# A state-space block on one core: the first part of y moves behind the first chunk of the next step

## The chip, the core and the metric

The kernel runs on one core of one Trainium2 chip. A core has TensorE (PE, matrix multiplication, with PEld for its weight loads), VectorE (DVE), ScalarE (ACT), GpSimd (POOL) and SyncE (SP, which here only issues DMAs). All share an on-chip memory; TensorE writes its results to PSUM banks, of which this kernel uses eight. Each engine works through its own instructions in order and waits for the others at semaphores. The metric is the device time of one execution in microseconds, lower is better. Times are medians over runs of the same kernel; a profile is one execution recorded by the hardware.

## What is computed

The input x has 64 sequences of 32 positions and 512 channels. The block is

- a conditioning: a small network makes from `cond_128` a 32x32 mixing matrix for each sequence, which mixes the 32 positions of x;
- a state-space layer on the result, added to x:

```
proj = hidden @ in_proj_w.T            # gate z 4096, conv part x 4096, B 1024, C 1024, dt 64
xBC  = silu(causal_conv4(proj[conv part]))
dt   = softplus(dt + dt_bias);  dA = exp(-exp(A_log) * dt)
for t in range(32):                    # state per head: 64 x 128; 64 heads in 8 groups
    state = state * dA[t] + (dt[t] * x[t]) (outer) B[t]
    y[t]  = state . C[t]
y    = rmsnorm_per_group(y + D * x) * norm_weight * silu(z)
out  = y @ out_proj_w.T
```

- a grouped convolution over channels and a gated dense layer, added again.

The kernel doesn't step through the 32 positions. For one group of eight heads it forms `C.B` for all pairs of positions (the Gram matrix), multiplies it with the decay between the two positions and with dt, and so gets a 32x32 matrix per sequence and head, with which y is one small matrix product.

## The kernel before

The 64 sequences are cut in four tiles of 16 sequences (T = 0 to 3; 512 columns each), and the 64 heads in eight groups (g = 0 to 7). The main loop (L923) has 32 **steps**, i = 8 T + g, one for each tile and group. A step works on ten **chunks** of the input projection (ORDER, L346): B, C, then x and z alternately four times. `chunk(i, c)` (L417) orders the loads of weights some chunks ahead and the splitting of a later weight tile, and does one chunk: 12 matmuls of 128x512 into one PSUM bank (`mm_split`, L193: each product is formed from a high and a low part, three times four matmuls). `evict` (L448) empties the bank: for z ScalarE's silu (L452), for the others a bias on ScalarE (L459), three taps of the convolution on VectorE (L463), and ScalarE's silu in place (L471). `flip` (L473) transposes an x chunk on VectorE into `xs` (L478); the fourth, `flip(i, 3)`, comes after chunk 9.

Beside that `gram` and `gram_rows` (L534, L549) form the Gram matrix, `scan` (L511) the decay, and `decay` (L561) puts both together in `src`, the tile that the page also shows as `y<-src,xs`. Then y: `y_part(i, a, e)` (L577) does the blocks a to e of 16. A block is 8 matmuls of 32 rows and 64 columns, two for each of four PSUM banks; `y_part(i, 0, 8)`, the **first part**, takes the four banks and does 64 matmul pairs, 128 in the profile's count of matmuls and as many weight loads; `y_part(i, 8, 16)`, the **second part**, does the rest. Each block needs all four x chunks of `xs`.

Step i also finishes step j = i - 1. After chunk 1 comes the second part of y of j and `yend(j, 0..3)` (L594), which reads the four y banks on ScalarE (square, L600) and VectorE (times z, L602) and splits the result in a high and a low part (L613, L614); after chunks 5 to 8 come the four output products `outp` (L675) of j, with `wo`, the output weights, and `outp_end` (L691), which adds them to `acc`.

In the first eight steps the weights come raw from memory and are split in a high and a low part by ScalarE and GpSimd (`w_split`, L401; `wo_split`, L664), and stored for the later tiles; from step 8 on the split tiles are loaded. Steps 5, 6 and 7 (and 13 to 15, 21 to 23) also prepare the next tile: `attend` and `cond` (the conditioning), `dt_stage` (softplus and decay). At the first step of a tile `da_store` and `da_load` (L341, L482) write the decay rows to memory and read them back spread out, by DMAs of SyncE.

The order on TensorE and SyncE is the order in which the program is written (`manual_schedule`, L906). The order on VectorE, ScalarE and GpSimd is set by a planner that simulates the program, and the waits are put in by it. All accumulators but one come from a pool of seven PSUM banks (`bank`, L89), used in turn: an allocation waits until the seventh one before it has been read.

After the loop (L1034) the last step's second part, its outputs and the dense layer follow, interleaved with `unit`, pieces of the second convolution (`conv`, L787).

Of the kernel before, what the change touches and what calls it, by code (L numbers as in the profile page):

```python
# [32 lines left out]
def mamba_block_kernel(  # L33
# [55 lines left out]
    def bank(name, rows=P, cols=TOK):  # L89
        return ps.tile([rows, cols], F32, tag="mm", name=name, bufs=7)  # L90
# [102 lines left out]
    def mm_split(o, a_hi, a_lo, b_hi, b_lo, n):  # L193
        last = 3 * n - 1
        j = 0
        for a, b in ((a_hi, b_hi), (a_lo, b_hi), (a_hi, b_lo)):
            for k in range(n):
                nc.tensor.matmul(o, lhsT=a(k), rhs=b(k), start=j == 0, stop=j == last)  # L198
                j += 1
# [141 lines left out]
    def da_store(T):  # L341
        m = m_of.pop(T)
        for g in range(NG):
            nc.sync.dma_start(out=da_d[T][g], in_=m[g:P:NG])
# [51 lines left out]
    def w_ahead(n):  # L396
        while ahead[0] <= n + (5 if ahead[0] < 10 * NG else 4 if n < 10 * NG else 6):
            w_load(ahead[0])
            ahead[0] += 1

    def w_split(n):  # L401
        if n >= NG * 10:
            return
        w = raws.pop(n)
        t = w_tile(n)
        hi, lo = t[:, 0], t[:, 1]
        if len(w.shape) == 4:
            hi, lo = (v.rearrange("p k (q c) -> p k q c", q=4) for v in (hi, lo))
        nc.scalar.copy(hi, w)  # L409
        sub_of[n] = nc.gpsimd.tensor_tensor(lo, w, hi.bitcast(F32), ALU.subtract).ins  # L410
        splits[n] = t
# [5 lines left out]
    def chunk(i, c):  # L417
        n = 10 * i + c
        g = i % NG
        kind, k = ORDER[c]  # L420
        st = state[i]
        for m, t in keep:
            nc.sync.dma_start(out=wsp_d[m], in_=t.bitcast(F32))
        keep.clear()
        w_ahead(n)
        with tc.issue_after(exp_of[0] if n == 0 else cast_of[0]):
            w_split(n + 3)
        w2 = splits.pop(n)
        if i < NG:
            keep.append((n, w2))  # L430
        hi, lo = w2[:, 0], w2[:, 1]
        hid_hi, hid_lo = hid_of[i // NG]
        o = bank(f"mm{n}")
        mm_split(
            o,
            lambda q: hi[:, q, :],
            lambda q: lo[:, q, :],
            lambda q: hid_hi[:, q, :],
            lambda q: hid_lo[:, q, :],
            KC,  # L440
        )
        tag, bufs = {"B": ("B", 2), "C": ("C", 2), "x": ("x", 4), "z": ("z", 6)}[kind]
        t = sb.tile([P, TOK], F32, tag=tag, name=f"{kind}{n}", bufs=bufs)
        st[(kind, k)] = t
        with tc.issue_after(exp_of[0]) if n == 0 else nullcontext():
            evict(i, c, o, t)

    def evict(i, c, o, t):  # L448
        g = i % NG
        kind, k = ORDER[c]  # L450
        if kind == "z":
            nc.scalar.activation(t, o, AF.Silu)  # L452
        else:
            if kind == "x":
                taps, bias = xw[k][:, g, :], xb[k][:, g : g + 1]
            else:
                cc = chunk_id(g, kind, k) - 32
                taps, bias = convw_s[:, cc, :], convb_s[:, cc : cc + 1]
            nc.scalar.activation(t, o, AF.Identity, bias=bias, scale=taps[:, 3:4])  # L459
            ov = o.rearrange("p (b t) -> p b t", t=L)  # L460
            tv = t.rearrange("p (b t) -> p b t", t=L)
            for d in (1, 2, 3):
                nc.vector.scalar_tensor_tensor(  # L463
                    tv[:, :, d:],
                    ov[:, :, : L - d],
                    taps[:, 3 - d : 4 - d],
                    tv[:, :, d:],
                    ALU.mult,
                    ALU.add,
                )  # L470
            nc.scalar.activation(t, t, AF.Silu)  # L471
# [105 lines left out]
    def y_part(i, a, e):  # L577
        st = state[i]
        if a == 0:
            st["y"] = [bank(f"y{i}_{q}") for q in range(4)]  # L580
        for n in range(a, e):
            hh, b = divmod(n, 8)
            for f in range(2):
                for q in range(4):
                    r = slice(32 * q, 32 * q + 32)
                    nc.tensor.matmul(  # L586
                        st["y"][q][64 * f : 64 * f + 64, 32 * n : 32 * n + 32],
                        lhsT=st["xs"][r, n, 2 * f : 2 * f + 2].rearrange("p e x -> p (e x)"),
                        rhs=st["dec"][r, 2 * hh + f, b, :],
                        start=True,  # L590
                        stop=True,
                    )
# [71 lines left out]
    def wo_split():  # L664
        if wo_raw:
            t, k, w = wo_raw.pop(0)
            nc.scalar.copy(t[:, 0, k, :], w)  # L667
            nc.gpsimd.tensor_tensor(t[:, 1, k, :], w, t[:, 0, k, :].bitcast(F32), ALU.subtract)

    def wo_store():  # L670
        if wo_new:
            g, t, h = wo_new.pop(0)
            nc.sync.dma_start(out=wos_d[g][:, h], in_=t[:, h].bitcast(F32))
# [213 lines left out]
    def unit(n=1):  # L887
        for _ in range(n):
            units.pop(0)()
# [33 lines left out]
    for i in range(NI):  # L923
        j = i - 1
        T, g = divmod(i, NG)
        state[i] = {}
        late = 2 if i == 0 else 0

        def step_more():
            next(cond_steps, None)  # L930
            next(dt_steps, None)

        def inner(c):
            nonlocal wo_steps
            if c in (1, 2, 3, 4):
                if c < 4:
                    wo_split()
                next(wo_steps, None)
            if c in (5, 6):
                wo_store()  # L940
            if i == 0 and c == 6:
                da_rows()
                scan(0)
            if i == 0 and c == 8:
                da_store(0)
            if c == (6 if i else 8) and i + 1 < NI and (i + 1) % NG:
                da_load(i + 1)
            if c == 8:
                wo_steps = wo_pieces(i)
                for _ in range(1 if i + 1 < NI else 4):  # L950
                    next(wo_steps)
            if c == 3 + late:
                gram(i)
            if c == 4:
                flip(i, 0)
                if i:
                    scan(i)
            if c == 7:
                gram_rows(i)
                decay(i)  # L960
            if i == NI - 1 and c > 4:
                p_more(1)

        chunk(i, 0)
        if i and g == 0:
            da_store(T)
            da_load(i)
        if i == 0:
            with tc.issue_after(sub_of[3]):
                setup_x(1)  # L970
        chunk(i, 1)
        inner(1)
        if i == 0:
            with tc.issue_after(sub_of[4]):
                setup_x(2)
        if j >= 0:
            y_part(j, 8, 16)
            yend(j, 0)
            yend(j, 1)
        chunk(i, 2)  # L980
        inner(2)
        if j >= 0:
            yend(j, 2)
            yend(j, 3)
        if i == 0:
            with tc.issue_after(sub_of[5]):
                setup_x(3)
                setup_skip()
        chunk(i, 3)
        inner(3)  # L990
        if j >= 0:
            sumsq(j)
        chunk(i, 4)
        inner(4)
        if g == 6 and T + 1 < NT:
            cond_steps = cond(T + 1)
        if g == 7 and T + 1 < NT:
            dt_steps = dt_stage(T + 1)
        chunk(i, 5)
        inner(5)  # L1000
        if j >= 0:
            out_step(j, 0)
        step_more()
        if g == 5 and T + 1 < NT:
            attend(T + 1)
            load_acc(T + 1)
        chunk(i, 6)
        flip(i, 1)
        inner(6)
        if j >= 0:  # L1010
            out_step(j, 1)
        next(dt_steps, None)
        chunk(i, 7)
        inner(7)
        if j >= 0:
            out_step(j, 2)
        step_more()
        chunk(i, 8)
        flip(i, 2)
        if j >= 0:  # L1020
            out_step(j, 3)
        inner(8)
        step_more()
        if i == NI - 3:
            turned_setup()
            ffn_start()
        chunk(i, 9)
        inner(9)
        flip(i, 3)
        next(dt_steps, None)  # L1030
        step_more()
        y_part(i, 0, 8)

    j = NI - 1  # L1034
    unit(1)
    y_part(j, 8, 16)
    unit(1)
# [213 lines left out]
```

## Time and profile before

| | |
|---|---|
| median of 3 runs | 1563.78 us (1557.54 to 1569.55) |
| profiled execution, whole | 1559.59 us |
| its span in the profile | 1557.8 us |
| granted TensorE clock over the span | 0.991 of full speed |
| TensorE busy / VectorE busy | 1512.2 us (97%) / 1179.9 us (76%) |
| all y matmuls busy, idle before them | 100.2 us / 22.0 us |
| a steady step, from first part to first part | 42.97 us |

The profile gives for every group of instructions the program line, the engine, the tile written and the tiles read (`y<-src,xs`), how many there are, the time they took and the idle time of the engine just before them, with what ended that idle time: an instruction of another engine, or "issue", where the instruction waited for nothing that the profile shows. Timelines list merged pieces by start and duration in microseconds from the span's start. Because matmuls overlap in the pipeline, a piece's duration runs some tenths of a microsecond into the next piece.

### The profile page before, as it was taken

How to read it: one execution, taken by the hardware profiler on the slowest of the kernel's cores; microseconds unless marked ns; L12 is line 12 of the kernel's file. 1: busy time of each engine (PE TensorE's matmuls, PEld its weight loads, DVE VectorE, ACT ScalarE, POOL GpSimd, SP SyncE). 2: the span in 40 equal slices, each digit the busy share in tenths (PEclk: the TensorE clock that was granted, in tenths of full speed). 3: DMA queues.
4: the chain of work that ended last, by engine and by line, in shares of the span. 5: the costliest groups of instructions: out<-in, count | busy, mean ns of one | idle time of the engine just before them, and what ended most of it. 6: DMA issues, size and time to landing. Idle time of an engine off the chain costs nothing.

```text
span 1557.8 us, 35832 instructions
## 1 busy us (share of the span) xinstructions
PE 1512.2 (97%) x14973; PEld 1243.4 (80%) x14973; DVE 1179.9 (76%) x1883; ACT 629.0 (40%) x1124; POOL 471.6 (30%) x446
## 2 busy tenths in 40 slices
PE   7799999999999999999999999999999999999898
PEld 5588887788788888888888888888888888888567
DVE  7578777789777777888877777887877777787568
ACT  5455555544433333344433433444433332333230
POOL 4666566553431221122241211223242211222210
PEclk9899999999999999999999999999999999999999
DMA  5677777876775555544675554554675555453455
GB/s 202 210 279 281 261 247 258 248 236 237 238 231 185 195 178 182 199 158 152 216 241 184 190 190 166 194 165 168 207 235 195 182 181 179 162 190 114 128 157 169
DMA packets 123585, 311.19 MB, mean 200 GB/s; under 512 B 30560, under 2 KB 42080, under 8 KB 121376
## 3 DMA queue, kind: packets, MB, share of 16 engines
q1 hardware_dynamic: 120608, 301.56, 57.3%
q0 software_dynamic: 2816, 7.34, 1.4%
q8 instruction: 118, 1.93, 0.5%
q14 instruction: 43, 0.35, 0.1%
HBM read 237.02 MB, written 71.83 MB: 198 GB/s over the span
## 4 chain that ended last, share of the span: by engine, by line
PE 69%; DVE 17%; issue 4%; POOL 3%; DMA 3%; ACT 2%; SPq 1%; POOLq 0%; ACTq 0%; DVEq 0%
PE mm L198 42%; PE o L198 17%; PE y L586 5%; DVE x L463 3%; DVE ylo L614 2%; POOL wsp L410 1%; PE g_ps L540 1%; DMA w<-in_win_dram 1%; DVE acc L696 1%; DVE src L531 1%; DVE src L570 1%; DMA wor<-in_wout_dram 1%; DVE C L463 1%; DVE z L602 1%; DVE xs L478 1%
## 5 line engine op out<-in xcount | busy, mean ns | idle before, releaser
L198 PE MATMUL mm<-hid,wsp 128*128 128x512 f32 x3840 | 922.9, 393 | 0.9 <-issue 0.9
L198 PEld LDWEIGHTS mm<-hid,wsp 128*128 128x128 f32 x3840 | 714.6, 188 | 148.5 <-issue 1.6
L610 POOL TENSOR_TENSOR y<-y,y 128x512 f32<-128x512 f32 x96 | 145.2, 1512 | 545.7 <-ACT y L600 540.7
L463 DVE SCALAR_TENSOR_TENSOR x<-mm,xw,x 128x496 f32<-128x496 f32 (+2 forms) x384 | 272.1, 709 | 24.8 <-ACT x L459 19.8
L198 PE MATMUL o<-wo,yhi 128*128 128x512 f32 x1024 | 276.9, 392 | 0.7 <-ACT wo L667 0.7
L471 ACT ACTIVATE x<-x 128x512 f32<-128x512 f32 x128 | 81.0, 632 | 389.8 <-DVE x L463 365.7
L198 PEld LDWEIGHTS o<-wo,yhi 128*128 128x128 f32 x1024 | 189.9, 188 | 39.0 <-ACT wo L667 1.1
L463 DVE SCALAR_TENSOR_TENSOR B<-mm,pack,B 128x496 f32<-128x496 f32 (+2 forms) x96 | 68.8, 717 | 173.8 <-ACT B L459 171.6
L614 DVE TENSOR_TENSOR ylo<-z,yhi 128x512 fp32r<-128x512 f32 x128 | 141.9, 1110 | 0.4 <-ACT yhi L613 0.4
L198 PE MATMUL o<-wo,ylo 128*128 128x512 f32 x512 | 137.0, 389 | 0.0
L459 ACT ACTIVATE x<-mm,xb,xw 128x512 f32<-128x512 f32 x128 | 99.6, 779 | 77.6 <-PE mm L198 76.8
L586 PEld LDWEIGHTS y<-src,xs 32*64 32x64 f32 x8192 | 91.8, 133 | 45.7 <-issue 30.3
L478 DVE STREAM_TRANSPOSE xs<-x 128x512 f32<-128x512 f32 x128 | 89.8, 701 | 45.6 <-ACT x L471 43.3
L586 PE MATMUL y<-src,xs 32*64 32x32 f32 x8192 | 100.2, 228 | 22.0 <-DVE xs L478 12.4
L696 DVE SCALAR_TENSOR_TENSOR acc<-o,r,acc 128x512 f32<-128x512 f32 x128 | 95.3, 744 | 34.7 <-POOL r L638 30.3
L638 POOL TENSOR_TENSOR r<-var,mhalf 128x4 f32<-128x4 f32 x32 | 32.9, 1028 | 274.0 <-DVE var L634 274.0
L198 PEld LDWEIGHTS o<-wo,ylo 128*128 128x128 f32 x512 | 96.1, 188 | 20.3
L602 DVE SCALAR_TENSOR_TENSOR z<-y,pack,z 128x512 f32<-128x512 f32 x128 | 94.5, 741 | 17.4 <-ACT y L600 17.4
L613 ACT CAST yhi<-z 128x512 fp32r<-128x512 f32 x128 | 78.8, 618 | 57.2 <-DVE z L602 57.0
L452 ACT ACTIVATE z<-mm 128x512 f32<-128x512 f32 x128 | 75.8, 592 | 49.1 <-PE mm L198 48.8
L410 POOL TENSOR_TENSOR wsp<-w,wsp 128x512 fp32r<-128x512 f32 x56 | 75.4, 1360 | 57.0 <-ACT wsp L409 45.6
L463 DVE SCALAR_TENSOR_TENSOR C<-mm,pack,C 128x496 f32<-128x496 f32 (+2 forms) x96 | 68.8, 716 | 16.1 <-ACT C L459 13.9
(204 smaller groups left out, 1352.8 us busy)
## 6 DMA issues: line engine op xcount, KB each, us to landing
wsp<-wsp SPq DMA_DIRECT2D x320, 512.0 KB, 4.0
wo<-wos SPq DMA_DIRECT2D x96, 512.0 KB, 4.9
wos<-wo SPq DMA_DIRECT2D x16, 1024.0 KB, 6.6
da<-da SPq DMA_DIRECT2D x124, 128.0 KB, 2.8
w<-in_win_dram SPq DMA_DIRECT2D x48, 256.0 KB, 5.3
wor<-in_wout_dram SPq DMA_DIRECT2D x32, 256.0 KB, 4.5
xr<-in_win_dram SPq DMA_DIRECT2D x24, 256.0 KB, 5.2
acc<-in_x_in_dram SPq DMA_DIRECT2D x4, 1024.0 KB, 5.6
```

The lines of the kernel that those rows point to most:

```text
L198: nc.tensor.matmul(o, lhsT=a(k), rhs=b(k), start=j == 0, stop=j == last)
L410: sub_of[n] = nc.gpsimd.tensor_tensor(lo, w, hi.bitcast(F32), ALU.subtract).ins
L459: nc.scalar.activation(t, o, AF.Identity, bias=bias, scale=taps[:, 3:4])
L463: nc.vector.scalar_tensor_tensor(tv[:, :, d:], ov[:, :, : L - d], taps[:, 3 - d : 4 - d], tv[:, :, d:], ALU.mult, ALU.add,)
L471: nc.scalar.activation(t, t, AF.Silu)
L478: nc.vector.transpose(st["xs"][:, :, k], t.rearrange("p (n t) -> p n t", t=L))
L586: nc.tensor.matmul(st["y"][q][64 * f : 64 * f + 64, 32 * n : 32 * n + 32], lhsT=st["xs"][r, n, 2 * f : 2 * f + 2].rearrange("p e x -> p (e ...
L602: nc.vector.scalar_tensor_tensor(z, y, nw_s[:, cc : cc + 1], z, ALU.mult, ALU.mult)
L610: st["add"] = nc.gpsimd.tensor_tensor(y2, st["y2"], y2, ALU.add).ins
L613: nc.scalar.copy(hi, z)
L614: st["lo"] = nc.vector.tensor_tensor(lo, z, hi.bitcast(F32), ALU.subtract).ins
L696: nc.vector.scalar_tensor_tensor(acc[:, bg, :], o, st["r"][:, bg : bg + 1], acc[:, bg, :], ALU.mult, ALU.add)
```

## The change

`y_part(i, 0, 8)` stood at the end of step i, behind chunk 9. Now it stands in step i + 1, behind that step's chunk 0, as `y_part(j, 0, 8)`; the last step's stands after the loop. On TensorE the order around the joint of two steps was: chunk 9, first part of y, chunk 0, chunk 1, second part. It becomes: chunk 9, chunk 0, first part, chunk 1, second part. The order of SyncE's instructions stays the same. The planner changes the order of the other engines a little: VectorE's in steps 1 and 2 alone, GpSimd's at six places of the first eight steps, and ScalarE's mostly by putting the silu of B before the bias of C.

```diff
         chunk(i, 0)
+        if i:
+            y_part(j, 0, 8)
         if i and g == 0:
             da_store(T)
             da_load(i)
...
         flip(i, 3)
         next(dt_steps, None)
         step_more()
-        y_part(i, 0, 8)
 
     j = NI - 1
+    y_part(j, 0, 8)
     unit(1)
     y_part(j, 8, 16)
     unit(1)
```

## The prediction

> **What bounds the kernel now.** I read the page first, then TensorE's waits, then its timeline at single steps, and last the DMA packets that carry instructions.
>
> ```profile
> PE 1512.2 (97%) x14973; PEld 1243.4 (80%) x14973; DVE 1179.9 (76%) x1883; ACT 629.0 (40%) x1124; POOL 471.6 (30%) x446
> q8 instruction: 118, 1.93, 0.5%
> PE 69%; DVE 17%; issue 4%; POOL 3%; DMA 3%; ACT 2%; SPq 1%; POOLq 0%; ACTq 0%; DVEq 0%
> ```
>
> TensorE is busy 97%, and most of the chain that ended last is its own. So a microsecond counts only if TensorE stops or starts again in it. Where does it stop? Its waits, with microseconds, times and longest:
>
> ```profile
> PE y L586 <- DVE xs L478: 12.4, 8, 4.7
> PE y L586 <- DVE src L570: 6.1, 1, 6.1
> ...
> PE y L586 <- issue: 3.5, 2, 3.2
> ```
>
> Nearly all of it stands before the y matmuls. A steady step (step 9; start, duration, then what):
>
> ```profile
> 475.88 2.88 PE L198 MATMUL mm<-hid,wsp 128*128 128x512 f32 x12
> 478.69 1.49 PE L586 MATMUL y<-src,xs 32*64 32x32 f32 x128
> 480.11 5.73 PE L198 MATMUL mm<-hid,wsp 128*128 128x512 f32 x24
> 485.77 1.49 PE L586 MATMUL y<-src,xs 32*64 32x32 f32 x128
> ```
>
> Chunk 9, first part of y, chunks 0 and 1 of the next step, second part of y, with no gap: VectorE's last transpose into xs ended 0.82 us before 478.69. In 22 of the 31 joints between steps it is like that, or with 0.1 us of waiting at most, so there the move can win nothing. Steps 0 and 5 are others:
>
> ```profile
> 50.65 5.60 PE L198 MATMUL mm<-hid,wsp 128*128 128x512 f32 x24
> 62.35 0.44 PE L586 MATMUL y<-src,xs 32*64 32x32 f32 x8 [6.10 <-DVE src L570]
> 67.53 1.98 PE L586 MATMUL y<-src,xs 32*64 32x32 f32 x120 [4.73 <-DVE xs L478]
> 69.44 7.41 PE L198 MATMUL mm<-hid,wsp 128*128 128x512 f32 x24
> ...
> 288.86 0.32 PE L586 MATMUL y<-src,xs 32*64 32x32 f32 x8
> 291.55 1.98 PE L586 MATMUL y<-src,xs 32*64 32x32 f32 x120 [2.38 <-DVE xs L478]
> 293.46 6.41 PE L198 MATMUL mm<-hid,wsp 128*128 128x512 f32 x24
> ```
>
> **What is removed.** Chunk 0 takes 2.72 us and now runs ahead of the first part, so a wait for xs of up to 2.72 + 0.82 us beyond the steady case is covered. I take a step's loss as the time from its first to its second part, less the steady 7.08 us. Step 5: 299.81 - 288.86 = 10.95, a loss of 3.87; in it are 0.7 us of half clock (the clock view shows 0.50 from 291.5 to 294.9, after 3.4 us with TensorE busy 1.07). Step 7 loses 4.09 likewise, step 4 1.32, step 6 1.16, steps 1, 13, 15, 23 and 3 together 1.66. In these steps xs was ready 8.3 us or less after the end of chunk 8; the moved part starts 5.37 + 2.72 = 8.09 us after it (9.9 in step 6). So all of these 12.1 us go, but for 0.1. In step 0 xs ends at 67.5 whatever TensorE does, and chunk 0 moves into the hole from 56.25: 2.72 us. The gain is **14.8 us**. What is late next is chunk 0's weight tile: from step 1 on it is split 14 us or more ahead of its use.
>
> **What is moved and costs nothing.** The call issues 128 matmuls and their weight loads, no DMA, so SyncE's and GpSimd's queues keep their order; ScalarE applies silu to B before it takes C's bias, both ready by then (3.0 and 4.1 us after chunk 0 ends). The y banks are taken one chunk later: the seven banks go round 19 times a step before and after; chunk 3 now waits for the eviction of chunk 0, 8 us earlier on TensorE and done in some 3. If such a cover fails, one bank wait appears per step. In step 8 TensorE already waits 0.7 us for the last piece of wo, which SyncE issues behind the store of da; without another delay up to 1.1 us of step 7's gain would come back there. I count 0, because the next item delays TensorE ahead of it.
>
> **What the trace of before hardly shows.** The two parts of y come to lie one chunk apart instead of two. Each part is 256 instructions (128 weight loads, 128 matmuls) in 1.42 us, and queue q8 brings TensorE's instructions: 118 packets of 16 KB for 30,308 instructions, one packet per 256. The tail has two parts of y only 2.8 us apart already:
>
> ```profile
> 1443.07 1.60 PE L586 MATMUL y<-src,xs 32*64 32x32 f32 x128
> 1444.60 2.80 PE L795 MATMUL cv<-pr,tww 32*32 32x512 f32 x48
> 1447.33 0.44 PE L586 MATMUL y<-src,xs 32*64 32x32 f32 x26
> 1450.98 1.25 PE L586 MATMUL y<-src,xs 32*64 32x32 f32 x102 [3.21 <-issue]
> ```
>
> TensorE stops 3.21 us in the middle of a part with nothing to wait for. Two more such stops, in the second parts of steps 6 and 20 (0.5 and 0.3 us), tell the rule. Counting TensorE's instructions from the start (weight loads, matmuls, semaphore waits), all three stops lie exactly at number 256 n + 449, with n the packet's number (23, 72, 110), and TensorE goes on 1.3 to 1.6 us after that packet's end. Packet n starts when TensorE has passed about number 256 n + 132, later by 2.9 us (median of the 20 packets called for in a first part in steps 9 to 30; 1.7 to 5.2), and takes 1.0. So 317 instructions must last 2.9 + 1.0 + 1.4 = 5.3 us. Called for within the first part, they reach into the second. Before, 52 of them are two chunks: 5.44 us and 265 at 180 per us, 6.9 us: enough. After, 26 are one chunk: 2.72 and 291 at 180 per us, **4.3 us: 1.0 us too little.** A call falls in that stretch for some 216 of 256 positions, about 26 of 31 steps. With each packet's own lateness, and about 0.8 us for each of the four that stood behind the packet before them, steps 9 to 30 give 15.5 us and steps 0 to 8, where DMA is busier, 8.5: **24 us lost.** The ends: 0, from the 27 second parts of the 31 steps that take 1.49 us now, and 37, with every packet as late as in this trace. The tail's 3.21 a step, the nearest row, is not taken 31 times: its packet started 4.9 us late, and one of those 20 was later. What queues behind the stop is everything on TensorE, so the cost is whole.
>
> [...]
>
> **Sum.** Span 1557.8 - 14.8 + 24 = 1567.0, with the 1.8 us around it 1568.8, against this execution's 1559.6: 9.2 us more. The median of the three runs, 1563.78, lies 4.2 us above the profiled execution, so I expect 1573.
>
> **Rivals.**
> 1. *Instructions arrive in time.* For: 27 of 31 second parts show 1.49 us, and step 22's packet came after 1.7 us, which would suffice. Against: the three stops at one number. Then only the gain stays: 1563.8 - 14.8 = 1549, the faster side. It decides for itself below 4.3 us from call to use.
> 2. *Packets come later still.* Four packets (called in steps 2, 6, 10, 20) stood behind the one before; if they stay as late (4.1, 3.4, 2.0 and 3.2 us of stop, not 3.3 in all), 9.4 are added, and 3 for half clock after the longest stops: 1585.
> 3. *VectorE holds steps 5 to 7.* It is busy 38.7, 39.2 and 43.4 us in steps that would shrink to 43.6, 48.2 and 45.6. If it can't close up, their waits (9.1 us) stay: 1582. Against: no wait of step 7 is seen in step 8, and B reaches VectorE earlier.
>
> **Numbers.** Forecast 0.50 (its own range 1564 to 1581), rival 1 0.18, rival 2 0.18, rival 3 0.14. A range from 1553 to 1588 leaves out most of rival 1 and the top of rival 2. Of 1% (15.6 us), about what a measurement can tell here: slower by more takes rivals 2 and 3 in most cases and the forecast's top, 0.33; faster by more needs rival 1 with nothing lost, 0.07; within 1% 0.60.
>
> **What would show it.** Right: waits of y for xs only in step 0, chunk 0 starting near 56 us, and 15 to 35 us of idle time by "issue" inside second parts, each stop at 256 n + 449, about 1 us, in some 26 steps. Wrong: second parts at 1.49 us throughout (rival 1), or y still waiting for xs in steps 5 to 7 (rival 3).

## The result, and the profile after

The changed kernel takes 1589.44 us in the median of six runs (1581.87 to 1593.52), the kernel before 1565.83 us in six runs beside it (1557.54 to 1569.55). The ratio is 1.015, with a 95% interval from 1.0128 to 1.0173: it is 1.5% slower. The forecast was 1573 and the range ended at 1588. The direction and the main loss were foreseen; a loss of some 15 us behind them was not.

The profiled execution took 1583.97 us, its span is 1582.2 us against 1557.8 before: 24.4 us more. The granted clock over the span fell from 0.991 to 0.987. From the page of the changed kernel, the busy times, the chain that ended last, and the group of the y matmuls (busy, mean ns, then the idle time ahead of them and what ended most of it):

```profile
PE 1524.5 (96%) x14973; PEld 1250.2 (79%) x14973; DVE 1183.6 (75%) x1883; ACT 634.9 (40%) x1124; POOL 469.7 (30%) x446
...
PE 84%; DVE 5%; issue 5%; POOL 2%; DMA 2%; SPq 1%; ACT 1%; POOLq 0%; ACTq 0%; DVEq 0%
...
L586 PE MATMUL y<-src,xs 32*64 32x32 f32 x8192 | 103.1, 227 | 29.8 <-issue 20.7
```

VectorE's share of the chain fell from 17% to 5%: the waits for xs are gone from it. TensorE's own share rose from 69% to 84%, and it is busy 12.3 us longer with the same 14973 matmuls: 9.2 us of that in the 128x512 matmuls of L198, which half clock lengthens (nine in 3.42 us at a granted clock of 0.50, sixteen in 3.43 us at 1.00, in the stretches below), and 2.9 us in the y matmuls. TensorE's waits in the changed kernel (total, times, longest):

```profile
PE y L586 <- issue: 20.7, 21, 3.0
PE y L586 <- DVE xs L478: 5.6, 2, 4.7
...
PE y L586 <- DVE src L570: 3.5, 1, 3.5
...
PE mm L198 <- issue: 3.0, 3, 2.0
PE o L198 <- ACT wo L667: 3.0, 2, 1.7
```

The waits of y for xs went from eight (12.4 us) to two (5.6 us). In their place stand 21 stops of y by "issue", 20.7 us, where there were two (3.5 us). The longest of them, 3.0 us, is in the tail, where the kernel before has one of 3.2 us; the others lie in the loop. TensorE's timeline around the joint of steps 5 and 6, which answers to the one with 10.95 us between the parts of step 5 before:

```profile
292.02 1.49 PE L586 MATMUL y<-src,xs 32*64 32x32 f32 x128
293.43 3.02 PE L198 MATMUL mm<-hid,wsp 128*128 128x512 f32 x12
296.38 1.79 PE L586 MATMUL y<-src,xs 32*64 32x32 f32 x128
```

First part, one chunk, second part; nothing waits for xs, and the second part has a small stop in it (1.79 instead of 1.49). A joint of a later step, between 11 and 12, which had no gap before:

```profile
569.90 1.49 PE L586 MATMUL y<-src,xs 32*64 32x32 f32 x128
571.32 3.02 PE L198 MATMUL mm<-hid,wsp 128*128 128x512 f32 x12
574.27 0.86 PE L586 MATMUL y<-src,xs 32*64 32x32 f32 x65
576.49 0.85 PE L586 MATMUL y<-src,xs 32*64 32x32 f32 x63 [1.36 <-issue]
577.27 5.96 PE L198 MATMUL mm<-hid,wsp 128*128 128x512 f32 x18
```

The second part stops in its middle. And the chunk behind it is slow: 18 matmuls in 5.96 us, where 24 take 5.73 at full clock. The view by stretches shows why (the second entry is TensorE's busy time, with its matmuls; the entry after POOL's is the granted clock):

```profile
574.14:577.55 3.41, 2.05 (x130) 1.78 (x130) 2.15 (x3) 0.94 (x2) 0.00 (x0) 1.00 0.64 203
577.55:580.97 3.42, 3.42 (x9) 2.65 (x9) 2.70 (x4) 2.95 (x6) 1.76 (x2) 0.50 0.29 113
```

In the stretch with the stop TensorE was busy 2.05 of 3.41 us, 1.71 of it with the small y matmuls; the next 3.42 us ran at half clock, nine matmuls, where the stretch after that had sixteen.

**The ledger.** I divided both profiles at the same matmuls: a *joint* runs from the start of chunk 9 to the start of the next step's chunk 2 and holds both parts of y, a *body* is the rest of a step.

| stretch | change, us |
|---|---|
| the 31 joints | +9.1 |
| half clock in the chunk behind the second part, joints 8, 11, 22 and 30 | +5.9 (1.59, 1.59, 1.25, 1.51) |
| step 8: outputs of step 7 wait for wo, then half clock | +4.2 |
| step 5: a stop of 2.05 us in chunk 3, behind the second part, then half clock | +3.4 |
| rest of the bodies | +1.4 |
| start and tail | +0.3 |
| sum (of unrounded parts) | +24.4 |

The joints alone are what the prediction had summed: 14.8 gained and 24 lost, 9.2 net; they measured 9.1. The bodies, which it had at zero, hold the missing 14.9. The stop of step 5, and the stretches ahead of it and behind it (the last two columns are the busy share of the DMA engines and GB/s):

```profile
256.48 2.56 PE L198 MATMUL mm<-hid,wsp 128*128 128x512 f32 x6 [2.05 <-issue]
...
249.87:253.28 3.41, 3.41 (x37) 2.84 (x24) 2.79 (x5) 2.88 (x6) 1.72 (x2) 1.00 0.96 327
253.28:256.70 3.42, 1.37 (x7) 0.98 (x6) 3.42 (x5) 2.59 (x5) 3.26 (x3) 1.00 1.05 417
256.70:260.10 3.40, 3.40 (x12) 2.90 (x11) 2.61 (x4) 1.03 (x2) 3.40 (x3) 0.50 0.32 131
```

### The profile page after: what moved, and what is told of

It reads as the page before. It is cut to its first block, busy times and chain, and to the rows that moved or that the text cites. A ratio compares the mean times of both kernels' runs of the same rounds, so it can differ in the third digit from the quotient of the medians.

```text
span 1582.2 us, 35863 instructions
## 1 busy us (share of the span) xinstructions
PE 1524.5 (96%) x14973; PEld 1250.2 (79%) x14973; DVE 1183.6 (75%) x1883; ACT 634.9 (40%) x1124; POOL 469.7 (30%) x446
## 4 chain that ended last, share of the span: by engine, by line
PE 84%; DVE 5%; issue 5%; POOL 2%; DMA 2%; SPq 1%; ACT 1%; POOLq 0%; ACTq 0%; DVEq 0%
PE mm L198 51%; PE o L198 21%; PE y L586 6%; PE g_ps L540 2%; PE cv L795 1%; POOL wsp L410 1%; PE gr_ps L552 1%; PE fo L198 1%; DMA wor<-in_wout_dram 1%; DMA w<-in_win_dram 1%; DVE fd L1140 1%; DVE fd L1139 1%; DVE x L463 1%; PE h_ps L217 0%; PE lo L198 0%
## 5 line engine op out<-in xcount | busy, mean ns | idle before, releaser
L198 PE MATMUL mm<-hid,wsp 128*128 128x512 f32 x3840 | 929.8, 395 | 3.0 <-issue 3.0
L198 PEld LDWEIGHTS mm<-hid,wsp 128*128 128x128 f32 x3840 | 718.4, 189 | 152.5 <-issue 3.7
L198 PE MATMUL o<-wo,yhi 128*128 128x512 f32 x1024 | 278.2, 393 | 3.0 <-ACT wo L667 3.0
L198 PEld LDWEIGHTS o<-wo,yhi 128*128 128x128 f32 x1024 | 190.4, 188 | 41.7 <-ACT wo L667 3.8
L614 DVE TENSOR_TENSOR ylo<-z,yhi 128x512 fp32r<-128x512 f32 x128 | 141.7, 1108 | 1.5 <-ACT yhi L613 1.3
L198 PE MATMUL o<-wo,ylo 128*128 128x512 f32 x512 | 138.0, 391 | 0.3 <-DVE ylo L614 0.3
L586 PE MATMUL y<-src,xs 32*64 32x32 f32 x8192 | 103.1, 227 | 29.8 <-issue 20.7
L198 PEld LDWEIGHTS o<-wo,ylo 128*128 128x128 f32 x512 | 96.4, 188 | 21.2 <-DVE ylo L614 0.8
L602 DVE SCALAR_TENSOR_TENSOR z<-y,pack,z 128x512 f32<-128x512 f32 x128 | 95.0, 743 | 20.7 <-ACT y L600 20.4
L600 ACT ACTIVATE y<-y 128x512 f32<-128x512 f32 x128 | 76.2, 597 | 45.8 <-PE y L586 44.8
```

The costliest lines, as they stand in the source:

```text
L586: nc.tensor.matmul(st["y"][q][64 * f : 64 * f + 64, 32 * n : 32 * n + 32], lhsT=st["xs"][r, n, 2 * f : 2 * f + 2].rearrange("p e x -> p (e ...
L600: nc.scalar.activation(y2, y, AF.Square)
L602: nc.vector.scalar_tensor_tensor(z, y, nw_s[:, cc : cc + 1], z, ALU.mult, ALU.mult)
L614: st["lo"] = nc.vector.tensor_tensor(lo, z, hi.bitcast(F32), ALU.subtract).ins
```

## The experiments

Ratios are to the kernel before, run on the same chip beside each. "Stops" are times over 0.2 us from one instruction's start to the next one's inside the second parts of the 31 joints, taken from the instruction records (a view of waits counts idle time of TensorE from 0.15 us, and the tail too, so its numbers differ a little); their position is counted in TensorE's instructions (weight loads, matmuls, semaphore waits) from the start.

### Both parts a chunk later

```diff
+        chunk(i, 2)
         if j >= 0:
             y_part(j, 8, 16)
             yend(j, 0)
             yend(j, 1)
-        chunk(i, 2)
         inner(2)
```

> The second part of y moves one chunk later too, behind chunk 2, so that two chunks lie between the parts again, as in the kernel before, while the first part keeps its cover of one chunk. Theory (instruction packets, and half clock in their wake): the stops at number 256 n + 449 shrink to three or fewer, 2 us in all or less, the four half clock windows behind them go, and the gain stays: about 14 us for the waits for xs, less some 4 us in step 8 (wait for wo and the half clock behind it), so a span of 1546 to 1551, ratio to the kernel before 0.992 to 0.996. Rival A (the loss belongs to the first part's new place, whatever lies between the parts): 1575 or more. Rival B (the seven banks go round once more tightly: chunk 4 waits for the eviction of the first y bank): up to 1 us more in each of 31 steps, 1560 to 1580, with waits of mm for y's evictions in the profile.

Measured: 1565.09 us, ratio 1.001 (0.9994 to 1.0027). The stops behaved as the theory said: none in 31 second parts, against 21 in the changed kernel. The joint of steps 9 and 10:

```profile
478.61 1.49 PE L586 MATMUL y<-src,xs 32*64 32x32 f32 x128
480.03 5.73 PE L198 MATMUL mm<-hid,wsp 128*128 128x512 f32 x24
485.69 1.49 PE L586 MATMUL y<-src,xs 32*64 32x32 f32 x128
```

And no half clock window stands behind a second part. The time, though, missed the expectation: the waits for xs are gone, but for 4.9 us in step 0 and 0.8 us in two later steps, and yet the kernel is no faster than the one before. Its waits show what came instead:

```profile
PE mm L198 <- issue: 3.1, 1, 3.1
...
PE o L198 <- DVE ylo L614: 2.3, 4, 0.9
...
PE o L198 <- DMA wo<-wos: 1.8, 1, 1.8
...
PE o L198 <- ACT yhi L613: 1.1, 1, 1.1
PE o L198 <- POOL wo L668: 0.9, 2, 0.7
```

The output matmuls, the next users of y, wait for a y that is finished a chunk later: 0.15 us in chunk 5 of a steady step, 4.1 us in that of step 7, half clock behind it included, and 3.3 us in that of step 16. In step 5 chunk 3 stops 3.1 us for instructions and loses 4.2. Against the first profile of the kernel before, with the time of the second part itself (1.51 us a step) left aside as it moves from joint to body, the joints won 13.9 us, the bodies lost 16.9, and start and tail lost 3.6. So the distance of the parts is shown to cause the stops; "the gain stays" was wrong.

### The second part a chunk earlier

```diff
         chunk(i, 0)
+        if j >= 0:
+            y_part(j, 8, 16)
...
-            y_part(j, 8, 16)
             yend(j, 0)
```

> The kernel before, with only the second part of y moved up behind chunk 0; the first part stays ahead of chunk 0, so the waits for xs stay and the parts lie one chunk apart as in the changed kernel. Theory (instruction packets): 20 to 27 of the 31 second parts stop, each at number 256 n + 449, 18 to 25 us in all; some of the longest (1.3 us and more) are followed by a half clock window of 3.4 us that costs up to 1.7 us each, 5 to 10 us in all; the waits for xs stay near 12 us. Span 1580 to 1592, ratio 1.014 to 1.022. Rival (the loss comes from the order of the first part and chunk 0, by the other engines): second parts of 1.49 us, span near 1558, ratio 1.00.

Measured: 1658.07 us, ratio 1.061 (1.0581 to 1.0643). The stops are there, 21 of them, 17.6 us, each at 256 n + 449. But a wait that neither theory had dwarfs them:

```profile
PE g_ps L540 <- ACT C L471: 55.1, 31, 2.8
PE y L586 <- issue: 15.5, 17, 2.7
```

The Gram matmuls wait for the silu of C in all steps but one, 1.8 us each. In steps 8 to 31 that silu ends 7.4 us after chunk 1 (median) instead of 3.8: y is finished a chunk earlier, and in the trace of step 12 its squares, products and splittings (L600, L602, L613, L614) stand among C's bias and taps on ScalarE and VectorE, where in the kernel before most of them come behind. As a price of the distance the run is spoiled; the count and place of the stops are not. That question went to the next run.

### The same distance at another place

```diff
         chunk(i, 0)
-        if i:
-            y_part(j, 0, 8)
...
         if j >= 0:
+            y_part(j, 0, 8)
+        chunk(i, 2)
+        if j >= 0:
             y_part(j, 8, 16)
```

The order is chunk 0, chunk 1, first part, chunk 2, second part.

> Chunk 0, chunk 1, first part of y, chunk 2, second part: the second part stands where e1_both_later has it, and the first part is moved one chunk further, so that one chunk lies between the parts again. Theory (instruction packets need 5.3 us for 317 instructions, wherever the parts stand): the stops are back, in 18 to 26 of 31 second parts, each at number 256 n + 449, 18 to 26 us in all, with some half clock behind the longest; span 25 to 40 us above e1_both_later, 1587 to 1605. Rival (the place behind chunk 0 was what cost): as e1_both_later, 1560 to 1568.

Measured: 1593.46 us in one run, span 1591.7, 27.3 us above the kernel with both parts a chunk later. 21 stops are back, 24.5 us, each at 256 n + 449:

```profile
PE y L586 <- issue: 22.1, 23, 2.0
```

With the second part at the same place and only the distance changed from two chunks to one, the loss is there. The rival, that the place behind chunk 0 costs, falls.

### Half as many instructions

```diff
-        for n in range(a, e):
+        for n in range(a, e, 2):
...
-                        st["y"][q][64 * f : 64 * f + 64, 32 * n : 32 * n + 32],
+                        st["y"][q][64 * f : 64 * f + 64, 32 * n : 32 * n + 64],
```

with two blocks of `dec` side by side as the moving operand. The second block of each pair gets the weights of the first, so this kernel computes something else and only its time is of use.

> The changed kernel, but each y matmul covers two of the 32-column blocks at once with the weights of the first, so a part has 128 instructions in place of 256 (the second block of each pair gets other numbers than it should; the rest of the work is the same). Theory (the number of instructions between the call and the stop decides): a call within the first part now reaches 317 instructions behind the second part at the earliest, so two chunks lie in between; no second part of the 31 in the loop stops, and no half clock window stands behind one. Span below that of the changed kernel by the stops and half clock (some 30 us) and by what the parts are shorter (0 to 44 us): 1508 to 1552. Rival (the time between the parts, or their array pattern, decides and not their instructions): stops in 15 or more second parts, 15 us or more.

Measured: 1520.12 us in one run, span 1518.3. No wait of y by "issue" is left. The joint of steps 9 and 10:

```profile
472.51 0.91 PE L586 MATMUL y<-src,xs 32*64 32x64 f32 x64
473.36 3.02 PE L198 MATMUL mm<-hid,wsp 128*128 128x512 f32 x12
476.31 0.91 PE L586 MATMUL y<-src,xs 32*64 32x64 f32 x64
```

The parts lie closer in time than in the changed kernel (3.80 us from start to start instead of 4.37) and nothing stops: time between the parts is not what decides, but the instructions in that time. 62 parts shorter by 0.57 us are 35 of the 64 us by which the span is below the changed kernel's. The joints are shorter by another 21.7 us, close to the 22.3 of the stops, and the tail by 5.4. The bodies are shorter by 1.9 only: the half clock behind the second parts (5.9) and the loss of step 5 are gone, but steps 6 to 8 take 7.5 us longer, with waits of the Gram matmuls for C and of the output matmuls for wo and ylo. Behind the hole of step 0, one half clock window is left in the loop, after the wait for wo in step 8.

### Only where it waits

The first part moves in steps 0, 1, 4, 5, 6 and 7 alone:

```diff
         chunk(i, 0)
-        if i:
+        if j in MOVED:
             y_part(j, 0, 8)
...
         step_more()
+        if i not in MOVED and i < NI - 1:
+            y_part(i, 0, 8)
```

> The first part moves behind chunk 0 only in steps 0, 1, 4, 5, 6 and 7, where it waits for xs in the kernel before; in the other steps it stays ahead of chunk 0. Theory: gain and loss add up step by step, so steps 9 to 30 take what they took before (no stop above 0.5 us there), and the first nine joints give what they gave in the changed kernel: 14 us of waits gone, 1 to 2 us of new stops in steps 4 and 5, up to 3.4 us for a late packet behind the second part of step 4, and up to 4 us in step 8. Span 1545 to 1555, ratio 0.992 to 0.998. Rival (the losses of the late steps are not the parts' distance but a state that the early steps leave behind, such as a later phase of the other engines): steps 9 to 30 lose part of the 20 us here too, 1560 or more.

Measured: 1560.34 us, ratio 0.9976 (0.9959 to 0.9993), span 1556.5. From joint 8 on every joint but two (0.36 us less in joint 20, 0.15 more in joint 21) is as before within 0.05 us, and of the bodies only two differ (0.7 and 0.8 us in chunk 5 of steps 16 and 24), so the loss is made step by step and leaves next to nothing behind; joints 20 and 21 and step 16 differ by the same amounts between the two profiles of the kernel before (below). In the early steps the ledger reads -2.8, -3.8 and -3.0 us in joints 0, 5 and 7, but +1.2 in joint 1 (a stop of 1.68, with 1.6 of half clock behind it), +0.6 in joint 6 (a stop of 1.64), and +3.7 in step 8. The ratio lies within what was expected, at its upper end, and the span 1.5 us above.

### The wait for wo

```diff
         if i and g == 0:
+            if T == 1:
+                next(wo_steps, None)
+                next(wo_steps, None)
             da_store(T)
             da_load(i)
```

> The changed kernel, but in step 8 two of the loads for wo are issued ahead of the store of da, so that the split of wo is done when the output matmuls come. Theory (the 4.0 us that step 8 loses behind its chunk 5 are 2.3 us more of waiting for wo, and half clock that this brings): the stretch of chunk 5 of step 8 falls from 10.5 to some 6.5 us, the half clock window near 410 us goes, all other joints are as in the changed kernel, the span 1576 to 1581. Rival (the half clock there comes from something else, or da is late in its stead and scan holds TensorE): the stretch, or the one behind it, stays 2 us or more longer.

Measured: 1580.13 us in one run, span 1578.3. First the changed kernel in step 8, then this one:

```profile
405.68 0.67 PE L198 MATMUL o<-wo,yhi 128*128 128x512 f32 x2
408.08 0.50 PE L198 MATMUL o<-wo,yhi 128*128 128x512 f32 x1 [1.73 <-ACT wo L667]
409.82 0.50 PE L198 MATMUL o<-wo,yhi 128*128 128x512 f32 x1 [1.24 <-ACT wo L667]
410.16 1.79 PE L198 MATMUL o<-wo,ylo 128*128 128x512 f32 x4
411.75 1.91 PE L198 MATMUL o<-wo,yhi 128*128 128x512 f32 x4
```

```profile
406.92 1.07 PE L198 MATMUL o<-wo,yhi 128*128 128x512 f32 x4
407.82 0.84 PE L198 MATMUL o<-wo,ylo 128*128 128x512 f32 x3
409.01 0.50 PE L198 MATMUL o<-wo,ylo 128*128 128x512 f32 x1 [0.35 <-DVE ylo L614]
409.35 1.09 PE L198 MATMUL o<-wo,yhi 128*128 128x512 f32 x4
```

The stretch of chunk 5 fell from 10.49 to 6.08 us, and the half clock behind it (four matmuls in 1.79 and 1.91 us instead of 1.07) is gone: the 4.2 us of step 8 were the last loads of wo behind the store of da. The other joints are not "as in the changed kernel": 20 stops, 25.7 us, of other sizes.

### The changed kernel again, and the kernel before again

> The changed kernel itself, profiled a second time. Theory (the position of a block's end is fixed by the program, the lateness of its packet is not): the same second parts stop, each at the same instruction, but by other amounts; those with the block's end near or behind their end stop in one profile and not in the other; the sum of the stops stays within 20 to 28 us, and the half clock windows behind them change places. Rival (the stops are fixed by the program): the same steps stop by the same amounts within 0.2 us.

Measured: 1595.22 us, span 1593.4. Again 21 stops, at the same instructions, 25.0 us, in 20 of the same 21 joints; but joint 1 now stops 2.34 us where it did not stop, joint 11 not at all where it stopped 1.58. Half clock stands behind other second parts (joints 1, 8, 10, 14, 26 and 28; only 8 is the same). The largest single difference is a chunk 2 of step 3 of 7.47 us instead of 3.80.

> The kernel before, profiled a second time, since the whole working stands on one profile of it whose time lies 4 us below the median. Theory (packets come late by chance in the kernel before too, and a stop of 1.5 us or more brings half clock): the same waits for xs in the same steps within 0.3 us; stops in the early steps and half clock behind them at other places, so that the two profiles differ by 3 to 10 us in steps 2 to 8 alone. Rival (the kernel before runs the same every time): span 1557 to 1559, each joint as in the first profile within 0.2 us.

Measured: 1565.24 us, span 1563.5, 5.7 us more than the first profile. The body of step 3 alone is 5.8 us longer, and what else differs cancels (the joint of steps 0 and 1, for one, is 1.6 us shorter, against an expectation of 0.3):

```profile
163.27 1.49 PE L586 MATMUL y<-src,xs 32*64 32x32 f32 x128
164.69 0.73 PE L198 MATMUL mm<-hid,wsp 128*128 128x512 f32 x2
169.49 6.80 PE L198 MATMUL mm<-hid,wsp 128*128 128x512 f32 x18 [4.06 <-issue]
```

This stop too lies at 256 n + 449 (n = 9); in the first profile the same instruction waited 0.7 us. So single packets come late in the kernel before as well, and one of its two profiles has 5 us more of it. Both theories' main points held: the place is fixed, the lateness is not. That a stop of 1.5 us or more brings half clock was not shown: in the first profile of the changed kernel one of 1.55 us (joint 18) brought none, and one of 1.48 us (joint 30) did.

### Towards a faster one

`e6_six_later` has both parts a chunk later in the same six steps, the outputs of these steps a chunk later, the loads of wo first, and in the tail two units between the parts; `e8_all_steps` has that in all steps.

```diff
+        if j in LATER:
+            y_part(j, 0, 8)
         chunk(i, 1)
...
         chunk(i, 2)
+        if j in LATER:
+            y_part(j, 8, 16)
...
-        if j >= 0:
+        if j in PLAIN:
             out_step(j, 0)
...
         chunk(i, 6)
+        if j in LATER:
+            out_step(j, 0)
...
-    unit(1)
+    unit(2)
     y_part(j, 8, 16)
-    unit(1)
```

> In steps 0, 1, 4, 5, 6 and 7, where the kernel before waits for xs, the first part stands behind chunk 0 and the second behind chunk 2; all other steps are as in the kernel before. The output matmuls of those steps begin one chunk later, two loads of wo go ahead of the store of da in step 8, and in the tail two units instead of one lie between the parts. Theory: no stop in any second part of the six steps, no wait of the output matmuls for ylo, yhi or wo; 12 to 14 us of waits gone, of which a late packet behind the second part of step 4 may take back up to 4; the tail 2 to 4 us shorter, as its stop of 3.4 us goes. Span 1540 to 1548, ratio 0.988 to 0.993. Rival (whatever is gained early is lost again at the next thing that is late, as in e1_both_later and e3_six_steps): 1554 or more.

> e1_both_later (first part behind chunk 0, second behind chunk 2, in every step), with the output matmuls beginning one chunk later in every step, two loads of wo ahead of the store of da in step 8, and two units between the parts in the tail. Theory (what e1_both_later lost again was the output matmuls waiting for ylo, yhi and wo behind a second part that comes 2.7 us later, and half clock behind these waits): the 0.15 us per step, the 4.1 us in step 7, 1.8 in step 8, 3.3 in step 16 and 1.3 in step 24 go, and the tail is 2 to 4 us shorter: 1543 to 1550, ratio 0.990 to 0.995. Rival (the later output matmuls hold the weights of wo longer, and the next load is late instead): 1558 or more, with waits of o for wo in every step.

Measured: 1564.38 us, ratio 0.9995 (0.9976 to 1.0014), and 1568.98 us, ratio 1.0031 (1.0015 to 1.0047). Both missed. In `e8_all_steps` no second part in the loop stops and no output matmul waits, but now y waits for xs:

```profile
385.59 0.31 PE L586 MATMUL y<-src,xs 32*64 32x32 f32 x6
386.36 0.27 PE L586 MATMUL y<-src,xs 32*64 32x32 f32 x2 [0.45 <-DVE x L463]
389.01 1.97 PE L586 MATMUL y<-src,xs 32*64 32x32 f32 x120 [2.38 <-DVE xs L478]
```

This is step 7, and steps 15 and 23 do the same; each of the three has half clock behind it. These are the steps in which VectorE also prepares the next tile; that it is late because it gets y and the outputs later fits, but was not tested. In `e6_six_later` no second part of the six steps stops by more than 0.11 us, but step 7 waits there too (0.8 us for x and 2.4 us for xs, with half clock behind), and packets come late elsewhere (in step 5's chunk 3 again, which loses 3.4 us, and in step 10's second part, 1.6 us, with half clock). In the tail most of the stop of 3.4 us turned into a wait of 3.1 us for a transfer, and the tail grew 3 us.

The last kernel keeps what the ledger of `e3_six_steps` shows as a net gain: steps 0, 5 and 7 moved, and the loads of wo first.

```diff
-    MOVED = (0, 1, 4, 5, 6, 7)
+    MOVED = (0, 5, 7)
```

> The first part moves behind chunk 0 only in steps 0, 5 and 7, where e3_six_steps showed more gain than stop, and in step 8 two loads of wo go ahead of the store of da; all else is as in the kernel before. Theory: gains of 2.8, 3.8, 3.0 and 1.0 us (step 8's own wait for wo), no new stop but a late packet here or there: 7 to 10 us less, span 1547 to 1552, ratio 0.992 to 0.997. Rival (a shifted phase of the blocks of 256 instructions makes other second parts stop, or a packet comes late in step 5, as in e6_six_later): 1555 or more.

Measured: 1555.96 us in the median of eight runs, against 1564.24 of the kernel before; ratio 0.9954 (0.9939 to 0.9970). That is 8 us less than the kernel before and the least of all kernels that compute the block. The ratio lies within what was expected; the span missed it (1553.0 to 1559.1 us in the eight runs, 1547 to 1552 expected). Its profile is of its slowest run (1560.86 us, span 1559.1), in which the rival came: joints 0, 5, 7 lower by 2.8, 1.3 and 3.8 us, but 3.5 us of a late packet in step 3, the one that the second profile of the kernel before has too, another late packet in step 5 (its body is 3.5 us longer), and a stop of 2.15 us, with half clock behind it, in the second part of step 5.

## Why the prediction was wrong, point by point

**The gain, 14.8 us: held, but for 1.1.** Waits for xs went in all the steps named except step 7, which keeps about 1.1 us (5.46 us between its parts instead of 4.37). "All of these 12.1 us go, but for 0.1" assumed that xs comes no later after chunk 8 than in the trace of before. In step 7 it came 9.19 us after the end of chunk 8 instead of 8.21. VectorE's timeline has the place:

```profile
380.27 0.70 DVE L478 STREAM_TRANSPOSE xs<-x 128x512 f32<-128x512 f32 x1
380.89 2.82 DVE L324 SCALAR_TENSOR_TENSOR dt<-dt 128x256 f32<-128x256 f32 x4
```

The same four instructions took 1.76 us before; a fifth, behind them, took 0.41 us instead of 0.88, so this is some 0.6 of the 1.0 us. What slowed them was not tested. The hole of step 0 was filled as foreseen (3.0 us).

**The loss by instruction packets, 24 us: held, in part by luck.** With 13.7 us gained and 9.1 net, the joints lost 22.8; the 21 stops sum to 22.3 (two of them, 0.8 us, stood in the kernel before), so 1.3 us of the loss belong to no stop. All lie at 256 n + 449, and TensorE went on 1.2 to 1.6 us after the packet's end, as said. The split was off in ways that cancel: 18.1 us in steps 9 to 30 (15.5 said), 4.1 in steps 0 to 8 (8.5 said); 21 stops instead of some 26, about 1.06 us each. Of the ten second parts without one, the call fell ahead of the first part in three (steps 2, 12 and 25), so that 7.0 to 8.5 us were left until the block's end; in six others (1, 7, 15, 23, 27 and 29) the packet started 1.3 to 2.3 us after the call, and in step 0 half clock left 6.1 us.

**The step that failed: what follows a stop was priced at nothing.** The forecast had no half clock behind the new stops; 3 us of it stood only in rival 2, "after the longest stops". Measured were 5.9 us behind four second parts, and part of the 4.2 us of step 8 and the 3.4 us of step 5, where half clock follows a longer wait and a stop too; together these are 13.5 of the missing 14.9 us. The kernels in which no second part stops (`e1_both_later`, `e7_half_the_matmuls`) have no such window behind one, and in the second profile of the changed kernel, where the stops have other sizes, the windows stand behind others of them. The row for it was at hand: in the kernel before, 3.4 us with TensorE busy 1.07 were followed by half clock. I read it as needing an almost idle stretch, though a second part with a stop of 1.0 to 1.5 us in it leaves some 0.5 to 1.0 us for large matmuls in 3.41 (estimated: less the stop and 1.42 us of small ones; measured 0.49 to 0.92 us in joints 8, 11, 22 and 30), and the small ones count for less (by the fit below).

**Two smaller zeros fell with it.** The wait for wo in step 8 was put at 0, "because the next item delays TensorE ahead of it". The joints up to step 7 gained more than they lost, TensorE came early, and the wait grew from 0.7 to 3.0 us, with half clock 4.2 us more; `e4_wo_first` took this away. And the count of the packets looked only into the second parts: the stop of step 5's chunk 3 lies at 256 n + 449 as well (n = 16), 39 instructions behind a second part. Its packet started 9.3 us after the call and 6.7 us after the end of the packet before, and the DMA engines were busy 0.96 to 1.05 of the time in the 10 us up to the stop. What makes this packet late was not tested; in the two profiles of the kernel before it was 6.3 and 7.0 us late and the same instruction stopped for 0.4 and 1.0 us, in the two of the changed kernel 9.3 us late both times, with stops of 2.2 and 2.7 us.

**The rivals.** Rival 1 (instructions in time) and rival 3 (VectorE holds steps 5 to 7, but for 1.1 us of step 7) did not come. Rival 2's number, 1585, is nearest to the profile's 1583.97, but not by its terms: the four packets it feared cost what they cost elsewhere. `e8_all_steps` shows that rival 3's limit is real and near.

**The offset to the median held**: 24.4 us between the first two profiles, 23.6 between the medians.

**Slips in the sums that decided nothing.** The terms of the gain add up to 14.7, not 14.8. All packets as late as in the trace of before cost 37 us in one place and 24 + 9.4 = 33 in rival 2. The seven banks don't go round 19 times a step: 19 is the number of allocations. No wait for a bank appeared.

**Most packets cost nothing that shows.** Of the 118 in the profile of the changed kernel, 21 stopped a second part in the loop, 22.3 us in all, where parts of 256 instructions in 1.42 us stand one chunk apart, and three a chunk, 3.0 us; two more stand in the tail, 3.0 us in y and 1.5 us in the convolution.

## What to carry to other kernels

Before bringing two bursts of small matmuls closer together, count the instructions between the call of a block and its end: here 317 of them must last 5.3 us (the prediction's estimate, 2.9 + 1.0 + 1.4 us from the trace of before), and the schedules that packed two bursts of 256 into less paid 0.8 to 1.3 us at each boundary that showed. Price a new stop together with what follows it: half clock in the next window (1.3 to 1.6 us each here), and the next wait that TensorE, now early or late, runs into. And move only where the trace shows a wait; moved in the 22 joints that had none, the part had nothing to win, and the stops of steps 9 to 30 cost 18.1 us.

## What the runs showed of the hardware

**Blocks of instructions.** Queue q8 brought 118 packets of 16 KB in both first profiles, for 30,308 instructions of TensorE before. In thirteen profiles of eleven kernels, every stop over 0.2 us inside a second part in the loop, 112 of them, lies at 256 n + 449, to the instruction. TensorE goes on 1.2 to 1.7 us after the packet's end. Packets are mostly prompt (median 3.2 us after the call, where TensorE passes about number 256 n + 132, in the kernel before, 3.5 in the changed one), but single ones start up to 11 us after it (13 in `e2_near`), and some are late again and again: packets 16 and 17, called for around the second y part of step 4, by 5.5 to 10.2 us in all twelve profiles with full y parts. Packet 9, called for near the y parts of step 2, was late by 3.5 us in one and 9.7 us in another.

**Half clock.** In the first profiles of the two kernels the granted clock is 1.00 or 0.50, and the stretches of 0.50 stand on one grid of 3.41 us: in the kernel before they begin 68, 97, 408 and 438 steps of 3.413 us behind the first, in the changed one 57, 102, 112, 151, 297, 401, 414 and 445. TensorE was not always idle ahead of one: in joint 11 it was busy 2.05 of 3.41 us. Over the 5180 full-clock windows between chunk 2 of step 1 and chunk 9 of step 31 in all thirteen profiles, with a microsecond of y matmuls counted as half (weight and threshold are fitted to these data), 53 of the 54 windows with at most 1.55 us of work were followed by half clock, and 2 of the 5126 with more. In the two first profiles these are eight of eight, with 0.74 to 1.49 us of work, and none with 1.65 us or more. A window behind a second part cost 1.3 to 1.6 us (joints 8, 11, 22 and 30). The length of the stop alone did not decide: stops of 1.48 and 1.55 us (joints 14 and 18) left 1.96 and 1.65 us of work, counted so, in their window and brought none, one of 1.48 us (joint 30) left 1.38 and did.
